# LayerNorm, causal attention and a ternary feed-forward block: gate and up of a batch in seven block products of 256 columns instead of eight

## The chip, the cores and the metric

The kernel runs on one core of a Trainium2 chip. A core has TensorE (matmul, called PE; its weight loads are shown as PEld), VectorE (DVE), ScalarE (ACT), GpSimd (POOL) and SyncE (SP), which run side by side and wait for each other by semaphores; SP, ACT and POOL also issue DMAs. Matmuls write to PSUM; the kernel's pools divide it into eight banks of 512 fp32 columns. The metric is the device time of one execution in microseconds (us), taken as the median of several runs.

## The reference

For x of 4 batches, 512 positions and 512 features:

```
xn = layernorm(x)                                   # per position, no scale or shift
s  = causal_attention(xn)                           # 16 heads of 128, W_Q, W_K, W_V, W_O, biases
g  = (xn @ gate_w.T) * gate_s                       # gate_w, up_w: 1408 x 512, entries -1, 0, 1
u  = (xn @ up_w.T) * up_s
f  = silu(((silu(g) * u) @ down_w.T) * down_s)      # down_w: 512 x 1408, entries -1, 0, 1
out = x + s * f
```

All is fp32. The kernel keeps fp32 accuracy by splitting an activation into a high part (rounded to fp32r, the type of the matmuls' operands) and the rest, a low part; a matrix of small whole numbers needs no low part.

## The kernel before

The x of all batches lies normalised and transposed in SBUF (`xnT`, per batch a high and a low tile of 128 x 4 x 512: four chunks of 128 features, 512 positions). The kernel has two stages, both with the order of instructions written out by hand (`manual_schedule`): on each engine they stand in the order in which the Python code issues them.

**Attention.** 64 heads (8 groups of 2 heads, 4 batches) run one after the other, each with scores and softmax (`softmax`), a transpose of p through VectorE and DRAM (`turn_p`, on SP's queue), the projection of the next head's q and k (`project`), v (`project_v`) and the output projection (`project_out`, which adds to `acc_d` in DRAM through the tiles `a`, in the last batch `a_last`, stored by SP at L499). GpSimd scales p (L371) and makes low halves of weights. Once a head, `look` ORs one tile of the ffn's weights into `bits` on VectorE (L529) and `load_look` loads the next on ScalarE's queue, 33 tiles in all: low bits in any of them would mean weights that need a low part. The answer is read into a register (L843), and the branch takes the exact path when there are none, which holds for these inputs.

**ffn.** `gate_up(b, f)` is called for 4 batches and 11 blocks f of 128 hidden features (L776). GpSimd's queue loads the two weight blocks (`fweight`, L754, six buffers each) and, in the second half of batch 0, the down weights `wd`. Per block, gate and up are 8 matmuls each of 128x128 weights by 512 columns (`mm`, L770: 4 chunks, high and low part), into PSUM tiles pg and pu of which there are two each. ScalarE makes silu(gate) (L794), VectorE multiplies with up (L796), ScalarE rounds to the high part (L800), VectorE subtracts for the low part (L801). After the first block of the next batch come the four tiles of `down` (L814): 22 matmuls of 512 columns each, and on the way out a product (L825, VectorE), a silu (L826, ScalarE), a product with the attention (L827) and the addition of x (L828), then SP's store (L829). Two PSUM banks hold the downs. The last batch's downs end the kernel, the last tile in two halves.

Of the kernel before, what the change touches and what calls it, by code (L numbers as in the profile page):

```python
# [10 lines left out]
F32 = mybir.dt.float32  # L11
F32R = mybir.dt.float32r
I32 = mybir.dt.int32
# [15 lines left out]
class Split:  # L29


    def __init__(self, hi, lo):
        self.hi, self.lo = hi, lo
# [10 lines left out]
def kernel(  # L44
# [44 lines left out]
    ]  # L89

    def mm3(ps, a, b, first, last):
        nc.tensor.matmul(ps, a.hi, b.lo, start=first, stop=False)  # L92
        nc.tensor.matmul(ps, a.hi, b.hi, start=False, stop=False)  # L93
        nc.tensor.matmul(ps, a.lo, b.hi, start=False, stop=last)  # L94
# [16 lines left out]

    with ExitStack() as at:
        lnp = at.enter_context(tc.tile_pool(name="lnp", bufs=NT))
        small = at.enter_context(tc.tile_pool(name="small", bufs=8))
# [17 lines left out]

        ident = const.tile([P, P], F32, name="ident")
        mask = const.tile([P, S], F32, name="mask")
        eps = const.tile([P, 1], F32, name="eps")

        def load_const(src, shape, name):
            t = const.tile(shape, F32, name=name)
            nc.gpsimd.dma_start(out=t, in_=src)
            return t  # L140
# [128 lines left out]

        v_of = {}  # L270

        def project_v(g, b, t):
# [6 lines left out]
            else:  # L279
# [8 lines left out]
                for c in range(ND):  # L288
                    nc.tensor.matmul(  # L289
                        ps[:, 1], x_[c].lo, wv[g].hi[:, c, :], start=False, stop=c == ND - 1  # L290
                    )
                rest = lnp.tile([P, D], F32, name="v_rest", tag="xn")[:, : HG * E]
                nc.scalar.copy(v.hi, ps[:, 0])
# [217 lines left out]

        n_ffn = 3 * NF
        bits = const.tile([P, D], I32, name="bits")
        looks, looking = list(range(n_ffn)), []

        def load_look():
            if looks:
                k = looks.pop(0)
                src = (gate_w, up_w, down_w)[k % 3][k // 3]
                if k % 3 < 2:  # L520
                    src = src.rearrange("p c i -> p (c i)")
                raw = lnp.tile([P, D], F32, name=f"look{k}", tag="xt")
                nc.scalar.dma_start(out=raw, in_=src)
                looking.append(raw)

        def look():
            if looking:
                raw = looking.pop(0)
                nc.vector.tensor_tensor(bits, bits, raw.bitcast(I32), ALU.bitwise_or)  # L529

        def low_bits():

            nc.vector.tensor_single_scalar(bits, bits, LOW_BITS, ALU.bitwise_and)
            low = const.tile([P, 1], F32, name="low")
            nc.vector.tensor_reduce(low, bits, AX.X, ALU.max)
            return low
# [9 lines left out]
        with tc.manual_schedule():  # L546
# [11 lines left out]
            nc.gpsimd.memset(bits, 0)  # L558
            ones = const.tile([P, 1], F32, name="ones")
            nc.gpsimd.memset(ones, 1.0)  # L560
# [41 lines left out]
            project_v(0, 0, 1)  # L602
            bo_bc = load_const(b_o.broadcast_to([P, D]), [P, D], "bo_bc")
            ds_bc = load_const(down_s.broadcast_to([P, D]), [P, D], "ds_bc")

            load_on[0] = nc.scalar
            heads = [(g, b, i) for g in range(NG) for b in range(B) for i in range(HG)]
            zs = {}
# [7 lines left out]
            for n, (g, b, i) in enumerate(heads):  # L616
# [69 lines left out]
                if g + 1 < NG:  # L686
# [5 lines left out]
                    if (b, i) == (B - 1, 0):  # L692
                        prepare_qk((g + 1) * HG + 1, (g + 1) * per_g - 1)
                look()
                if g > 0:
                    load_look()
                if before is not None:
# [22 lines left out]
                if n == len(heads) - 4:  # L720
                    assert not looks and not looking
                    low = low_bits()
# [7 lines left out]

# [110 lines left out]
    with tc.If(flag == 0) as cond:  # L844
        ffn(True)
    with cond.Else():
# [60 lines left out]
```

## Time and profile before

| what | us |
|---|---|
| median of 3 runs (1206.56 to 1209.08) | 1207.38 |
| the profiled execution | 1208.75 |
| its span, first to last instruction | 1207.0 |
| start of the ffn on TensorE | 960.23 |
| end of the last matmul's turn on TensorE | 1200.15 |
| from there to the end of the span | 6.85 |
| busy in the ffn's 239.92 us: TensorE / VectorE / ScalarE | 239.91 / 95.81 / 68.75 |

The profile is one execution. Rows of the chain and of timelines give a start from the beginning of the span and a length in us, then engine, line (L770 is line 770 of the kernel), operation, output<-inputs by name, shape and count; brackets give how long the engine had idled and what ended that. Rows of groups give the busy time and the mean ns of one. Matmuls overlap: one of 512 columns is shown 389 ns long, but starts follow each other more closely.

### The profile page before, as it was taken

How to read it: one execution, taken by the hardware profiler on the slowest of the kernel's cores; microseconds unless marked ns; L12 is line 12 of the kernel's file. 1: busy time of each engine (PE TensorE's matmuls, PEld its weight loads, DVE VectorE, ACT ScalarE, POOL GpSimd, SP SyncE). 2: the span in 40 equal slices, each digit the busy share in tenths (PEclk: the TensorE clock that was granted, in tenths of full speed). 3: DMA queues.
4: the chain of work that ended last, by engine and by line, in shares of the span. 5: the costliest groups of instructions: out<-in, count | busy, mean ns of one | idle time of the engine just before them, and what ended most of it. 6: DMA issues, size and time to landing. Idle time of an engine off the chain costs nothing.

```text
span 1207.0 us, 18482 instructions
## 1 busy us (share of the span) xinstructions
PE 1194.2 (99%) x6018; PEld 1021.9 (85%) x6018; DVE 841.8 (70%) x2261; ACT 549.8 (46%) x1272; POOL 366.9 (30%) x484
## 2 busy tenths in 40 slices
PE   8999999999999999999999999999999999999997
PEld 8888888888888888888888888888888888888886
DVE  7987778787778777777777777777777543443433
ACT  6654444455445545444544454555544331323231
POOL 3312332343235323332523252335231350202110
PEclk9999999999999999999999999999999999999999
DMA  4465456666665667666766665655555992737241
GB/s 163 141 186 149 145 163 206 196 191 193 192 209 180 204 196 220 183 198 201 218 186 183 182 191 171 187 176 175 175 159 169 299 297 80 218 79 219 78 149 38
DMA packets 117912, 215.52 MB, mean 179 GB/s; under 512 B 13232, under 2 KB 45744, under 8 KB 117808
## 3 DMA queue, kind: packets, MB, share of 16 engines
q1 hardware_dynamic: 73872, 134.38, 35.2%
q10 hardware_dynamic: 29520, 53.40, 15.7%
q0 software_dynamic: 14416, 26.48, 8.2%
q8 instruction: 50, 0.82, 0.3%
q14 instruction: 54, 0.44, 0.1%
HBM read 135.17 MB, written 79.04 MB: 177 GB/s over the span
## 4 chain that ended last, share of the span: by engine, by line
PE 94%; DVE 3%; DMA 1%; ACT 1%; issue 0%; SPq 0%; ACTq 0%; DVEq 0%
PE psq L104 14%; PE psk L104 14%; PE psv L285 9%; PE z L452 8%; PE sc L104 8%; PE pd L770 7%; PE pg L770 7%; PE pu L770 7%; PE pso L92 5%; PE pso L93 5%; PE pso L94 5%; PE psv L289 4%; PE psv L104 1%; PE sc L342 1%; DVE sq L385 1%; DVE st L213 1%
## 5 line engine op out<-in xcount | busy, mean ns | idle before, releaser
L371 POOL TENSOR_SCALAR p<-p,rtot 128x512 f32<-128x512 f32 (+3 forms) x256 | 135.3, 547 | 603.0 <-DVE rtot L368 578.6
L365 ACT ACTIVATE p<-p,nmax 128x512 f32<-128x512 f32 (+3 forms) x256 | 140.8, 552 | 137.3 <-DVE nmax L351 137.3
L285 PE MATMUL psv<-wv,xh 128*128 128x512 f32 x448 | 124.7, 400 | 0.0
L104 PE MATMUL sc<-k,q 128*128 128x512 f32 (+2 forms) x576 | 112.6, 338 | 2.5 <-DVE xl L261 1.8
L385 DVE STREAM_TRANSPOSE sq<-p 128x256 f32<-128x256 f32 x378 | 113.4, 365 | 0.0
L104 PEld LDWEIGHTS sc<-k,q 128*128 128x128 f32 x576 | 99.0, 188 | 14.3 <-ACT xh L260 1.5
L351 DVE CUSTOM_DVE_ANT_0 p<-sc,mask 128x512 f32<-128x512 f32 (+2 forms) x192 | 96.3, 552 | 0.0
L308 ACT ACTIVATE k<-psk,consts 128x512 fp32r<-128x512 f32 (+1 forms) x65 | 44.3, 681 | 106.0 <-PE psk L104 106.0
L418 ACT CAST pt<-ptr 128x640 fp32r<-128x640 f32 x126 | 85.1, 724 | 13.2 <-DMA ptr<-turn 8.5
L309 DVE SCALAR_TENSOR_TENSOR k<-psk,consts,k 128x512 fp32r<-128x512 f32 (+1 forms) x65 | 48.1, 740 | 61.2 <-ACT k L308 60.8
L420 POOL TENSOR_TENSOR pt<-ptr,pt 128x640 fp32r<-128x640 f32 x53 | 83.7, 1579 | 13.3 <-ACT pt L418 10.3
L285 PEld LDWEIGHTS psv<-wv,xh 128*128 128x128 f32 x448 | 76.0, 188 | 10.0
L796 DVE SCALAR_TENSOR_TENSOR hd<-pu,consts,sg 128x512 f32<-128x512 f32 x44 | 33.0, 751 | 66.8 <-PE pu L770 62.2
L289 PEld LDWEIGHTS psv<-wv,xl 128*128 128x128 f32 x448 | 68.4, 188 | 9.5
L420 DVE TENSOR_TENSOR pt<-ptr,pt 128x640 fp32r<-128x640 f32 x73 | 69.9, 968 | 3.0 <-ACT pt L418 3.0
L498 DVE TENSOR_TENSOR a<-pso,a 128x512 f32<-128x512 f32 x108 | 69.8, 685 | 3.0 <-PE sc L343 1.7
L289 PE MATMUL psv<-wv,xl 128*128 128x256 f32 x448 | 71.0, 280 | 0.0
L368 DVE RECIPROCAL rtot<-tot 128x1 f32<-128x1 f32 x256 | 41.4, 162 | 41.2 <-ACT p L365 35.1
L308 ACT ACTIVATE q<-psq,consts 128x512 fp32r<-128x512 f32 (+1 forms) x65 | 44.2, 681 | 42.4 <-PE psq L104 41.8
L452 PE MATMUL z<-pt,v_0h 128*128 128x512 f32 x128 | 50.6, 395 | 0.0
L309 DVE SCALAR_TENSOR_TENSOR q<-psq,consts,q 128x512 fp32r<-128x512 f32 (+1 forms) x65 | 47.8, 735 | 3.9 <-ACT q L308 3.9
L365 ACT ACTIVATION_READ_ACCUMULATOR p<-p,nmax 128x1 f32 x256 | 47.8, 187 | 0.0
(717 smaller groups left out, 3037.3 us busy)
## 6 DMA issues: line engine op xcount, KB each, us to landing
turn<-sq SPq DMA_DIRECT2D x63, 640.0 KB, 2.9
ptr<-turn SPq DMA_DIRECT2D x252, 160.0 KB, 5.2
acc<-a SPq DMA_DIRECT2D x124, 256.0 KB, 2.5
a<-acc ACTq DMA_DIRECT2D x108, 256.0 KB, 3.3
xt<-in_x SPq DMA_DIRECT2D x16, 256.0 KB, 4.3
wor<-in_w_o ACTq DMA_DIRECT2D x16, 256.0 KB, 6.2
fa<-acc SPq DMA_DIRECT2D x16, 256.0 KB, 5.8
fx<-in_x SPq DMA_DIRECT2D x16, 256.0 KB, 5.9
```

The costliest lines, as they stand in the source:

```text
L104: nc.tensor.matmul(ps, l, r, start=n == 0, stop=n == len(todo) - 1)
L285: nc.tensor.matmul(ps, x_[c].hi, wv[g].both[:, :, c, :], start=c == 0, stop=False)
L289: nc.tensor.matmul(ps[:, 1], x_[c].lo, wv[g].hi[:, c, :], start=False, stop=c == ND - 1)
L308: nc.scalar.activation(q.hi[:, at_], ps, AF.Identity, bias=bias[:, h : h + 1])
L309: nc.vector.scalar_tensor_tensor(q.lo[:, at_], ps, bias[:, h : h + 1], q.hi32[:, at_], ALU.add, ALU.subtract)
L351: nc.vector.tensor_tensor_reduce(out=of[t], in0=where[t], in1=add, scale=-SCALE, scalar=BIG, op0=ALU.add, op1=ALU.min, accum_out=nmax[t],)
L365: nc.scalar.activation(of[t], of[t], AF.Exp, bias=nmax[t], scale=-1.0, accum_out=tot)
L371: nc.gpsimd.tensor_scalar(of[t], of[t], rtot, 1.0, ALU.mult, ALU.mult)
L385: nc.vector.transpose(dst.rearrange("p a s i -> p s a i"), src.rearrange("p (s a i) -> p s a i", s=n, i=Q),)
L420: on.tensor_tensor(dst(pt.lo), src, dst(pt.hi32), ALU.subtract)
L452: nc.tensor.matmul(o, v, p_, start=k == 0, stop=k == len(todo) - 1)
L770: nc.tensor.matmul(ps, l, r, start=first and k == 0, stop=last and k == len(pairs) - 1)
```

## The change

Take the weights of a block as a 2x2 matrix of blocks (gate and up by the first and second half of the features: g1, g2, u1, u2) and a batch of x likewise (b11, b12, b21, b22: halves of features by halves of positions). Gate and up of the batch are the product of both, which takes eight block products; the new code forms sums of blocks and takes seven, after Winograd. The weights' sums s1 to s4 are small whole numbers; x's sums t1 to t4 are split anew into high and low.

The attention makes the weights' sums: `look` and `load_look` become `chores`, one step a head. In four heads it loads gate and up of a block, ORs gate and makes the four sums of 128x256 on GpSimd while it loads the down block, ORs up and the first sums tile and stores both tiles through SP into `sum_d`, and ORs the second. The sums are looked at as well. `v_rest` becomes one tile for all calls; constants of the attention alone move to a pool that ends with it.

The ffn of exact weights is new, `ffn_exact`; the other path stays. Each unit (b, f) is a list of pieces with a time in slots, seven slots to a unit; pieces with times past 7 fall into the next units, and a list sorted by time issues them. `plain` is the old pair of products, in two slots' positions; PLAIN says how many units of each batch are so (4, 1, 0, 0). `seven` is the new form. Its PSUM tile px collects four products in turn, copied out by ScalarE after the first three (s1, u2, u3); pz takes two, py one. VectorE adds the pieces: sg0 (gate, first half of positions), c22, sg1 (gate, second half). c22 must be read from pz before the product in slot 11 adds to it.

`sums_of(b)` makes x's sums: 13 steps on VectorE of 128x512 and 4 roundings on ScalarE. For batch 0 they stand among its plain units, for batch 1 all at once ahead of the first down, for batches 2 and 3 one at slots 2.5 and 5.5 of the units f = 2 to 8 of the batch before. A unit loads, on GpSimd's queue, gate, half of up and the sums (896 KB instead of 512), in batch 0 one down block more after each unit's own weights.

```diff
--- before.py
+++ after.py
+    sum_d = [dram.tile([P, 2 * D], F32, name=f"sum{f}", tag=f"sum{f}") for f in range(NF)]
...
-                rest = lnp.tile([P, D], F32, name="v_rest", tag="xn")[:, : HG * E]
+                if not v_rest:
+                    v_rest.append(lnp.tile([P, D], F32, name="v_rest", tag="xn"))
+                rest = v_rest[0][:, : HG * E]
...
-        def load_look():
...
-        def look():
...
+        def chores():
+            sums = [lnp.tile([P, D], F32, name=f"sums{k}", tag="xn") for k in range(2)]
+            h_ = D // 2
+            d = []
+            for f in range(NF):
+                g = load_look(gate_w[f].rearrange("p c i -> p (c i)"), f"lookg{f}")
+                u = load_look(up_w[f].rearrange("p c i -> p (c i)"), f"looku{f}")
+                look(*d)
+                yield
+                look(g)
+                s1, s2, s3, s4 = (t[:, c : c + h_] for t in sums for c in (0, h_))
+                for o, l, r, op in (
+                    (s1, u[:, :h_], u[:, h_:], ALU.add),
+                    (s2, s1, g[:, :h_], ALU.subtract),
+                    (s3, g[:, :h_], u[:, :h_], ALU.subtract),
+                    (s4, g[:, h_:], s2, ALU.subtract),
+                ):
+                    nc.gpsimd.tensor_tensor(o, l, r, op)
+                d = [load_look(down_w[f], f"lookd{f}")]
+                yield
+                look(u, sums[0])
+                for k in range(2):
+                    nc.sync.dma_start(out=sum_d[f][:, ts(k, D)], in_=sums[k])
+                yield
+                look(sums[1])
+                yield
+            look(*d)
+            found.append(True)
...
-                look()
                 if g > 0:
-                    load_look()
+                    next(chore)
...
+    def ffn_exact():
...
+            ps_y = ff.enter_context(tc.tile_pool(name="ps_y", bufs=1, space=PSUM))
+            ps_z = ff.enter_context(tc.tile_pool(name="ps_z", bufs=2, space=PSUM))
+            ps_d = ff.enter_context(tc.tile_pool(name="ps_d", bufs=2, space=PSUM))
+            N2, D2 = S // 2, ND // 2
+            PLAIN = (4, 1, 0, 0)
...
+            def sums_of(b):
+                (b11, b12), (b21, b22) = blk[b]
...
+                steps = (
+                    (p, b12.hi32, b11.hi32, ALU.subtract),
+                    (q, low(b12), low(b11), ALU.subtract),
+                    (p, p, q, ALU.add),
+                    (t1, p),
+                    (q, b22.hi32, p, ALU.subtract),
+                    (q, q, low(b22), ALU.add),
+                    (t1.lo, p, t1.hi32, ALU.subtract),
+                    (t2, q),
+                    (p, b21.hi32, q, ALU.subtract),
+                    (p, p, low(b21), ALU.add),
+                    (t2.lo, q, t2.hi32, ALU.subtract),
+                    (t4, p),
+                    (q, q, b11.hi32, ALU.subtract),
+                    (q, q, low(b11), ALU.subtract),
+                    (t4.lo, p, t4.hi32, ALU.subtract),
+                    (b12, q),
+                    (b12.lo, q, b12.hi32, ALU.subtract),
+                )
+                for o, *of in steps:
+                    if len(of) == 1:
+                        nc.scalar.copy(o.hi, *of)
+                    else:
+                        dve(o, *of)
+                        yield
...
+            def load_down(k):
+                wd[k] = wdp.tile([P, D], F32R, name=f"wd{k}", tag=f"wd{k}")
+                nc.gpsimd.dma_start(out=wd[k], in_=down_w[k])
+            def load(src, shape, tag, bufs=None):
+                t = fw.tile(shape, F32R, name=tag, tag=tag, **({"bufs": bufs} if bufs else {}))
+                nc.gpsimd.dma_start(out=t, in_=src)
+                return t
+            def product(ps, w, x_, more=False):
+                todo = [
+                    (w[:, c, :], part[:, c, :])
+                    for part in (x_.hi, x_.lo)
+                    for c in range(w.shape[1])
+                ]
+                for k, (l, r) in enumerate(todo):
+                    nc.tensor.matmul(
+                        ps, l, r, start=not more and k == 0, stop=k == len(todo) - 1,
+                        skip_group_check=more,
+                    )
+            def leave_hid(b, hd):
+                s = Split(
+                    hp.tile([P, S], F32R, name="hh", tag="hh"),
+                    hp.tile([P, S], F32R, name="hl", tag="hl"),
+                )
+                hid.setdefault(b, []).append(s)
+                nc.scalar.copy(s.hi, hd)
+                yield
+                nc.vector.tensor_tensor(s.lo, hd, s.hi32, ALU.subtract)
+            def times(o, up, f, sg):
+                nc.vector.scalar_tensor_tensor(
+                    o, up, us_sb[:, f : f + 1], sg, ALU.mult, ALU.mult
+                )
...
+            def plain(b, f):
+                g = load(gate_w[f], [P, ND, P], "wg")
+                u1 = load(up_w[f][:, :D2], [P, D2, P], "wu1", 2)
+                u2 = load(up_w[f][:, D2:], [P, D2, P], "wu2", 4)
+                pg = ps_x.tile([P, S], F32, name="pg", tag="x")
...
+            def seven(b, f):
...
+                g = load(gate_w[f], [P, ND, P], "wg")
+                u2_ = load(up_w[f][:, D2:], [P, D2, P], "wu2", 4)
+                s_ = load(sum_d[f][:, : 3 * D2 * P].rearrange("p (c i) -> p c i", i=P),
+                          [P, 3 * D2, P], "ws")
+                s4 = load(sum_d[f][:, 3 * D2 * P :].rearrange("p (c i) -> p c i", i=P),
+                          [P, D2, P], "ws4", 4)
+                s1, s2, s3 = (s_[:, k * D2 : (k + 1) * D2] for k in range(3))
+                px = ps_x.tile([P, N2], F32, name="px", tag="x")
+                pz = ps_z.tile([P, N2], F32, name="pz", tag="z")
+                made = {}
+                def temp(name):
+                    made[name] = fp.tile(
+                        [P, N2], F32, name=name, tag=name, bufs=1 if name in ("s1", "u3") else 2
+                    )
+                    return made[name]
+                def plus(o, ps, t):
+                    nc.vector.tensor_tensor(temp(o), ps, made[t], ALU.add)
+                def at0():
+                    product(px, g[:, :D2], b11)
+                    nc.scalar.copy(temp("s1"), px)
+                def at1():
+                    py = ps_y.tile([P, N2], F32, name="py", tag="y")
+                    product(py, g[:, D2:], b21)
+                    plus("sg0", py, "s1")
+                def at3():
+                    product(px, s2, t2, True)
+                    nc.scalar.copy(temp("u2"), px)
+                    silu(made["sg0"], f)
+                def at5():
+                    product(pz, s1, t1)
+                def at6():
+                    product(px, s3, t3, True)
+                    nc.scalar.copy(temp("u3"), px)
+                def at8():
+                    plus("c22", pz, "u3")
+                def at9():
+                    product(px, u2_, t4, True)
+                    made["hd"] = fp.tile([P, S], F32, name="hd")
+                def at10():
+                    times(made["hd"][:, :N2], px, f, made["sg0"])
+                def at11():
+                    product(pz, s4, b22, True)
+                    plus("sg1", pz, "u2")
+                def at13():
+                    silu(made["sg1"], f)
+                def at14():
+                    times(made["hd"][:, N2:], made["c22"], f, made["sg1"])
+                    made["left"] = leave_hid(b, made["hd"])
+                def at16():
+                    next(made["left"])
+                def at17():
+                    next(made["left"], None)
+                return [
+                    (0, at0), (1, at1), (3, at3), (5, at5), (6, at6), (8, at8), (9, at9),
+                    (10, at10), (11, at11), (13.5, at13), (15.5, at14), (17.5, at16), (19, at17),
...
+            class Down:
+                def __init__(self, b, t, c=slice(0, D), store=nc.sync, o=None):
+                    self.b, self.t, self.c, self.store = b, t, c, store
+                    self.o = fp.tile([P, D], F32, name="o") if o is None else o
+                    self.ps = ps_d.tile([P, c.stop - c.start], F32, name="pd", tag="pd")
+                def add(self, ff_):
+                    for f in ff_:
+                        h_ = hid[self.b][f][:, ts(self.t, P)]
+                        for part in (h_.hi, h_.lo):
+                            nc.tensor.matmul(
+                                self.ps, part, wd[f][:, self.c],
+                                start=f == 0 and part is h_.hi,
+                                stop=f == NF - 1 and part is h_.lo,
+                            )
+                    return self
+                def leave(self, last=True):
+                    a, xt = tail_in[self.b, self.t]
+                    silu_product(self.o, self.ps, self.c, a, xt)
+                    self.store.dma_start(
+                        out=out[self.b, ts(self.t, P), self.c], in_=self.o[:, self.c]
+                    )
...
+                units = [(b, f) for b in range(B) for f in range(NF)]
+                for k, (b, f) in enumerate(units):
+                    at_ = 7 * k
+                    if b > 0 and f == 1:
+                        run(at_)
+                        for e in [e for e in events if e[2] == k - 2]:
+                            events.remove(e)
+                            e[1]()
+                        if b == 1:
+                            sums = sums_of(b)
+                            advance()
+                        for t in range(NT):
+                            Down(b - 1, t).add(range(NF)).leave()
+                            if t + 3 < NT:
+                                load_tail(b - 1, t + 3)
+                    if f < PLAIN[b]:
+                        unit = plain(b, f)
+                        if b == 0:
+                            advance((6, 3, 2, 1)[f])
+                    else:
+                        if b == 0 and f == PLAIN[b]:
+                            advance()
+                        unit = seven(b, f)
+                    if b == 0:
+                        load_down(f)
+                    if 0 < b < B - 1 and f == 2:
+                        sums = sums_of(b + 1)
+                    if 0 < b < B - 1 and 2 <= f < 9:
+                        unit = sorted(
+                            unit + [(2.5, lambda: advance(1)), (5.5, lambda: advance(1))],
+                            key=lambda e: e[0],
+                        )
+                    events += [(at_ + n, what, k) for n, what in unit]
+                    run(at_ + 7)
+                    if f == NF - 1:
+                        for t in range(3):
+                            load_tail(b, t)
...
-        ffn(True)
+        ffn_exact()
```

## The prediction

> **What bounds the kernel now.** I began with the busy times of the page:
>
> ```profile
> PE 1194.2 (99%) x6018; PEld 1021.9 (85%) x6018; DVE 841.8 (70%) x2261; ACT 549.8 (46%) x1272; POOL 366.9 (30%) x484
> ```
>
> TensorE works 99% of the span, so time is won only by giving it less to do, and lost by every gap opened on it. Next the chain that ended last, in order of time, for the ffn:
>
> ```profile
> 960.23 2.08 PE pg L770 x8
> 962.31 1.81 PE pu L770 x8
> 964.13 1.81 PE pg L770 x8
> ...
> 1004.02 19.95 PE pd L770 x88
> ...
> 1179.91 20.24 PE pd L770 x110
> ```
>
> The ffn begins at 960.2; a gate or an up of 8 matmuls of 512 columns takes 1.813 us (226.7 ns each), the four tiles of a down 19.95. Nothing stands between these rows. What a 256-column matmul costs back to back is in the timeline of TensorE near the start:
>
> ```profile
> 13.77 0.64 PE L104 MATMUL psv<-wv,xh 128*128 128x256 f32 x4
> ...
> 18.09 0.64 PE L104 MATMUL psv<-wv,xh 128*128 128x256 f32 x4
> 18.57 0.40 PE L104 MATMUL sc<-k,q 128*128 128x512 f32 x1
> ```
>
> Forty start between 13.77 and 18.57: 4.80/40 = 120 ns. (The last down agrees: 20.24 less 66 x 0.2267 leaves 5.28 for 44, 120 ns.) Half the columns cost 53% of the time.
>
> Three more views set the prices of gaps. First the weight queue (timeline of POOL) and, below it, SP's stores of the last attention sums:
>
> ```profile
> 956.28 0.53 POOL L754 DMA_DIRECT2D wu5h<-in_up_w  x1 [0.45 <-DMA wu1h<-in_up_w]
> 965.41 0.53 POOL L754 DMA_DIRECT2D wd0h<-in_down_w  x1 [8.60 <-DMA fx<-in_x]
> ```
> ```profile
> 955.89 4.44 SPq L499 DMA_DIRECT2D acc<-a_last  x4
> ```
>
> The first down weight, wd0, lies where the attention's last tiles lay: it waits 8.6 us, until the stores of `a_last` (last issue 960.0) have landed. Today twelve gate and up loads stand ahead of it in the queue. Then VectorE and ScalarE after the last tile of a down (timelines):
>
> ```profile
> 1083.85 0.69 DVE L825 TENSOR_TENSOR o<-pd,ds_bc 128x512 f32<-128x512 f32 x1 [2.18 <-PE pd L770]
> 1085.23 0.69 DVE L827 TENSOR_TENSOR o<-o,fa 128x512 f32<-128x512 f32 x1 [0.70 <-ACT o L826]
> 1085.96 0.69 DVE L828 TENSOR_TENSOR o<-o,fx 128x512 f32<-128x512 f32 x1
> ```
> ```profile
> 1084.57 0.63 ACT L826 ACTIVATE o<-o 128x512 f32<-128x512 f32 x1 [4.36 <-DVE o L825]
> ```
>
> TensorE left the down at 1083.64; VectorE is held by this chain until 1086.65, 3.0 us, ScalarE until 1085.20. Today nobody needs them. Last, a 256-wide addition out of PSUM (groups, shapes apart):
>
> ```profile
> L294 DVE TENSOR_TENSOR v_rest<-psv,v_0h 128x256 f32<-128x256 f32 x25 | 10.6, 425 | 2.3
> ```
>
> [...] here the granted clock fell about 2.7 us after the last matmul. A gap of 3.9 could pay for that[...]; it goes into the range.
>
> **The change part by part.** *Products.* A plain pair has 16 x 226.7 = 3.63 us; seven products of 4 matmuls have 28 x 120 = 3.36. PLAIN keeps 4+1 pairs, so 39 change: 39 x 0.266 = **-10.4 us**. Downs, tail and last output are as before.
>
> *Attention.* 33 looks become 55 (22 x 0.75 = 16.5 us of VectorE), there are 44 sums of 128x256 on GpSimd and 22 stores on SP. A head lasts 14.6 us of unbroken TensorE; in 600 to 629 us VectorE was busy 23.7 of 29.2. Five looks in four heads instead of four add 0.2 us a head, at most 0.75 at once. The sums follow the weight halves in GpSimd's queue and precede the next head's scaling of p, for which GpSimd waits 603 us in all; at 1.58 us for 640 (pt, L420) four of 256 are 2.5 us, an estimate. SP's stores wait for sums made one head earlier. I take 0; at worst an uncovered look in eleven heads, +8, which nothing suggests.
>
> *(a) Start.* The queue is now gate, up, up, wd0 of unit 0, and only then unit 1's gate. wd0 still waits for `a_last`, but with three loads instead of twelve ahead the stores should land in 2.5 us (the median of acc<-a), near 962.5. Unit 1's gate issues at 963 and lands after the 2.9 to 3.0 us of an uncrowded load: 966. TensorE wants it at 960.2 + 3.63 = 963.9. Gap **2.0 us**: at least 1.0 (a store of 2.0), at most 5 (wd0 at 965.4 as today).
>
> *(b) x's sums of batch 1.* All 13 VectorE steps are issued ahead of the first down's output. From the end of the plain unit (T0): its two products, a cast and a subtraction, and the last seven unit's product, cast and subtraction, reach T0+4.2. Thirteen steps at 0.61 to 0.73 (most read what the step before wrote) end at 13.2; the first down then leaves PSUM at 13.8. The third down needs that bank (two of them) at T0+10.0. Gap **3.9**, 2.5 to 5. What is late next, the second down's exit at 16.5, precedes the fourth down's need at 18.9.
>
> *(c) Joints after a down.* With the 3.0 us chain at the head of both queues: ScalarE's copy s1, needed before the fourth product of the unit, ends at 1.9 instead of 1.05, so that product starts at 2.0 instead of 1.44; the eleventh-slot product next needs VectorE's c22, which starts at 3.0 and ends 3.4: another 1.0. So 1.6 for batches 2 and 3; for batch 1, whose previous unit is plain, only s1 and u2: 1.1. **4.3**, from 2 to 5.
>
> *(d) x's sums of batches 2 and 3 among the products.* A seven unit asks VectorE for three additions (0.425), two products (0.49, extrapolated from 618 ns for 384 and 749 for 512) and one subtraction of 0.69: 2.94. In the trace waiting instructions start about 0.08 before the one ahead ends (three L498 in 1.88 us): 2.46. Two x-sums of 0.61 make 3.68 against 3.36: 0.32 late per unit, for 6.5 units 2.1, of which about 0.7 fits into the time by which u3 and c22 come early. **1.4 a batch, 2.8**. Below: 0. Without overlap 4.32: 0.96 x 6.5 - 0.5 = 5.7 a batch, 11.4. ScalarE has three copies (0.37), two silus (0.47), one cast (0.62): 2.67 of 3.36, hidden.
>
> *(e) Latencies in a unit.* A product's result is out 0.64 us after its start, a copy takes 0.37 and two slots are 0.96; where a silu lies ahead of s1 the margin is 0.15. I take 0.3 for the first seven unit and 0.6 for the rest, **0.9**; 0 to 4.
>
> *DMA.* Four or five issues of 0.53 us a unit: 2.7 of 3.36. In batch 0 a unit loads 1152 KB = 1.18 MB, 3.0 us at the 390 GB/s seen between 960 and 983: hidden; at 292 GB/s (mean of 960 to 1000) 4.04, +0.68 x 7.
>
> Sum: -10.4 + 2.0 + 3.9 + 4.3 + 2.8 + 0.9 = **+3.5 us**. The profiled execution took 1208.75 (span 1207.0 and 1.75 around it): 1212.3. The median of the runs is 1.37 lower: **1210.9**.
>
> **The rivals.** *VectorE keeps up* (other side): x's sums cost nothing, (b) and (d) vanish, -3.2: 1204.2. It decides where the sums cost under 3.2 us in all (the rest of the gaps is 7.2 against 10.4). For it: the down leaves VectorE 13 us of 20. Against: 0.69 a step, and the order of the queue. *VectorE becomes the bound*: no overlap, (d) 11.4: 1219.5. Against: starts closer than durations. *Weights become the bound in batch 0*: +4.8: 1215.7. For it: DMA was busy 98% from 960 to 1000; against: TensorE did not wait then. *256 columns don't pay*: bound by the 188 ns of a weight load, 28 x 0.188 = 5.26, +64 us; the 120 ns rule it out.
>
> **How the numbers follow.** Forecast 0.45 (by itself 1207 to 1214), VectorE keeps up 0.27, VectorE the bound 0.13, weights 0.12, others 0.03. The range 1203 to 1219 leaves out the quickest part of the second and the slowest of the last. 0.2% (2.4 us) is about what can be told from no change. Faster 0.28 (most of the second case, a little of the first), same 0.14, slower 0.58.
>
> **What would show it.** Rows of 28 matmuls in 3.36 us; a gap of about 2 us before unit 1's gate, with wd0 issued near 962.5; one of about 4 before the third down of batch 0, released by o<-pd; two of 0.5 and 1.0 after each later down, released by s1 and c22; VectorE over 95% busy while sums run. An unbroken TensorE at these places, a 256-column matmul far from 120 ns, or a longer attention would make it wrong.

## The result: 1.1% slower, where 0.3% was forecast

| what | before | after |
|---|---|---|
| median, us | 1207.34 (1206.56 to 1209.08) | 1221.35 (1220.01 to 1222.06) |
| ratio to before | | 1.0113, interval 1.0098 to 1.0128 |
| profiled execution / its span, us | 1208.75 / 1207.0 | 1221.51 / 1219.7 |
| start of the ffn on TensorE | 960.23 | 960.02 |
| first gate matmul to last matmul, starts | 239.63 | 253.00 |
| from the start of the last matmul to the end | 7.12 | 6.72 |

The direction was right and the time was not: 1221.35 lies above 1210.9 and above the range's end, 1219. The attention is as long as before; all of the loss is in the ffn. One of the five runs of `wd_late` below took 3029.11 us, for a reason that is not known, and stays out of its median. On the page TensorE is still busy 98% of the span, but the row of the granted clock has an 8 in two places of the ffn:

```profile
PE 1194.8 (98%) x6486; PEld 1040.9 (85%) x6486; DVE 944.8 (77%) x2496; ACT 599.8 (49%) x1449; POOL 447.3 (37%) x611
...
PEclk9999999999999999999999999999999898999999
```

TensorE's waits in the ffn of the changed kernel (engine, line, what it waited for: total, times, longest, in us):

```profile
PE pg L874 <- DMA wg<-in_gate_w: 5.4, 1, 5.4
PE pd L1025 <- DVE o L766: 4.0, 2, 3.7
PE px L874 <- ACT s L953: 2.8, 4, 1.5
PE pz L874 <- DVE c L949: 1.6, 2, 0.8
```

These are the waits that the prediction names in (a), (b), (c) and (e). The first is far longer than forecast. To size each place with what follows it, I took the starts of all matmuls of the ffn and subtracted 0.2267 us for each of 512 columns and 0.120 for each of 256; what is left over is lost time.

| place | forecast | left over in the trace |
|---|---|---|
| 39 units in seven products | -10.4 | -10.4 |
| (a) before unit 1's gate | 2.0 | 5.5, and 1.9 in the matmuls after it |
| (b) before the third down of batch 0 | 3.9 | 3.8, and 3.0 in the matmuls after it |
| (c) joints after a down, batches 1, 2, 3 | 1.1, 1.6, 1.6 | 1.2, 1.6, 1.6 |
| (d) units with x's sums | 1.4, 1.4 | 1.0, 1.1 |
| (e) other units | 0.9 | 2.0, all in unit (0,4) |
| end, last batch's downs | 0 | 0.8 |
| sum | +3.5 | +13.1 |

The ffn grew by 13.4. The chain of waits of the changed kernel shows the start:

```profile
962.53 0.52 POOL wd L859
963.05 6.18 DMA wg<-in_gate_w
...
969.27 3.78 PE pg L874 x8
973.06 1.93 PE pu L874 x8
974.99 1.82 PE pg L874 x8
...
978.62 1.81 PE pg L874 x8
...
990.51 0.48 PE py L874 x4
...
993.87 0.48 PE py L874 x4
```

The lower rows give the first row of the table: a plain unit takes 978.62 - 974.99 = 3.63 us and a seven unit 993.87 - 990.51 = 3.36 where nothing interrupts them, and 39 units have changed.

wd0 went out at 962.53 and unit 1's gate at 963.05, as forecast (962.5 and 963). But the gate took 6.18 us to land, not 3.0. And its 8 matmuls took 3.78 us where eight of a later unit took 1.82: half speed. At the third down the same chain has

```profile
1024.38 0.69 DVE o L766
...
1025.12 13.10 PE pd L1025 x44
...
1076.40 19.99 PE pd L1025 x88
```

Two tiles of a down cost 13.10 us, where four of the next batch cost 19.99, so two should cost 10.0. Busy times by stretch (columns: stretch, length, busy time and instructions of PE, PEld, DVE, ACT, POOL, then granted clock, DMA share, GB/s) say why:

```profile
1021.00:1024.00 3.00, 0.44 (x2) 0.01 (x1) 2.79 (x5) 1.24 (x2) 0.00 (x0) 1.00 0.00 0
1024.00:1026.00 2.00, 0.89 (x2) 0.79 (x3) 1.30 (x3) 0.63 (x1) 0.00 (x0) 0.57 0.00 0
1026.00:1029.00 3.00, 3.00 (x8) 2.33 (x8) 2.27 (x4) 0.63 (x1) 0.00 (x0) 0.50 0.26 90
...
1031.00:1034.00 3.00, 3.00 (x15) 2.45 (x14) 0.69 (x1) 0.02 (x1) 0.00 (x0) 0.98 0.16 59
```

TensorE idles from 1021.4 on, the clock halves at 1024.3, and it stays at 0.50 until 1031.1, 6 us after work has resumed; 8 matmuls fall into 3 us where 15 do after 1031. "Busy" hides this: a slow matmul counts as busy. So there are two open questions: why the gate landed late, and whether the half speed is the price of the gap before it.

### The profile page after: what moved, and what is told of

It reads as the page before. It is cut to its first block, busy times and chain, and to the rows that moved or that the text cites. A ratio compares the mean times of both kernels' runs of the same rounds, so it can differ in the third digit from the quotient of the medians.

```text
span 1219.7 us, 20216 instructions
## 1 busy us (share of the span) xinstructions
PE 1194.8 (98%) x6486; PEld 1040.9 (85%) x6486; DVE 944.8 (77%) x2496; ACT 599.8 (49%) x1449; POOL 447.3 (37%) x611
## 5 line engine op out<-in xcount | busy, mean ns | idle before, releaser
L427 DVE TENSOR_TENSOR pt<-ptr,pt 128x640 fp32r<-128x640 f32 x73 | 76.6, 1060 | 2.6 <-ACT pt L425 2.6
L1025 PE MATMUL pd<-wd,hh 128*128 128x512 f32 (+1 forms) x187 | 71.6, 388 | 4.0 <-DVE o L766 4.0
L1025 PE MATMUL pd<-wd,hl 128*128 128x512 f32 (+1 forms) x187 | 71.3, 386 | 0.0
L863 POOL DMA_DIRECT2D ws<-sum x78 | 41.6, 543 | 36.4 <-PE px L874 33.4
L863 POOL DMA_DIRECT2D wg<-in_gate_w x44 | 24.0, 546 | 78.2 <-PE py L874 68.1
```

Of the source, the lines that this page charges most:

```text
L427: on.tensor_tensor(dst(pt.lo), src, dst(pt.hi32), ALU.subtract)
L1025: nc.tensor.matmul(self.ps, part, wd[f][:, self.c], start=f == 0 and part is h_.hi, stop=f == NF - 1 and part is h_.lo,)
```

## The experiments

Medians below stand beside 1221.35 of the changed kernel. The ratios stand against the kernel before on the same chip: 1207.98 for the first four kernels told of here, 1207.29 for `joints`, `unit_04` and `tuned_2`, 1207.68 for the rest. The kernel before thus moves by 0.7 us from chip to chip, and differences of less than about 1 us between medians are not read here.

### The start: place in the queue or crowded engines

```diff
-                    if b == 0:
-                        load_down(f)
+                    if b == 0 and f > 1:
+                        for j in (2 * f - 4, 2 * f - 3) if f < 4 else (f,):
+                            load_down(j)
```

> One edit to the changed kernel: in batch 0 the first down weight is loaded after the weights of unit 2 and not after those of unit 0 (two each in units 2 and 3, one in each later unit). Theory, place in the queue: unit 1's gate waits only because it stands behind wd0, which waits for the stores of a_last. Then the gap of 5.5 us before unit 1's gate goes, and with it the half clock that follows it (1.9 us): 1221.35 - 7.4 = 1213.9 us. Rival, crowding: the DMA engines are full from 960 to 975 whatever the order, because fa and fx and the weights come together; then unit 2's up (whose tile is free only at 964) is late in place of unit 1's gate, by 2 to 5 us: 1216 to 1221.

Measured: 1213.67, -7.7; ratio 1.0045 (1.0029 to 1.0061). The gap before unit 1's gate is gone, and nothing came in its place at unit 2. So without the gate's place behind wd0 there is no gap. (The profiled execution also lost 1.7 us more in unit (0,4), where the clock now fell, and 1.2 less than the changed kernel after the third down.) What made 5.5 of the forecast 2.0 is the question of the next run.

```diff
             def load_tail(b, t):
+                queue = nc.gpsimd if b == 0 and t < 3 else nc.sync
                 a = fa.tile([P, D], F32, name="fa")
-                nc.sync.dma_start(out=a, in_=acc_d[b][t])
+                queue.dma_start(out=a, in_=acc_d[b][t])
                 xt = fa.tile([P, D], F32, name="fx")
-                nc.sync.dma_start(out=xt, in_=x[b, ts(t, P), :])
+                queue.dma_start(out=xt, in_=x[b, ts(t, P), :])
```

> One edit to the changed kernel: the six loads of fa and fx for batch 0's downs (1.57 MB, issued by SyncE from 960.5 on) go to GpSimd's queue, behind the last weights of batch 0; wd0 stays ahead of unit 1's gate. It takes the landing time apart from the queue's place. If the 6.2 us that unit 1's gate needed from issue to landing come of sharing the DMA engines with fa and fx, it lands in the 3.0 us that I had predicted, at 966.1: gap 2.3 instead of 5.5, [...]so 3.2 + 1.9 = 5.1 us less: 1216.2. If they come of GpSimd's own five loads in a row, the gate still lands after 968 and the time stays within 1 us of 1221.3.

Measured: 1219.27 (1216.39 to 1220.68), -2.1. The order of wd0 and the gate is untouched. Timelines of GpSimd and, below it, of TensorE in this run, at the start and at the end of batch 0:

```profile
962.55 0.55 POOL L863 DMA_DIRECT2D wg<-in_gate_w  x1
```
```profile
962.78 0.61 PE L874 MATMUL pu<-xl,wu 128*128 128x512 f32 x2
965.68 1.19 PE L874 MATMUL pg<-xh,wg 128*128 128x512 f32 x4 [2.28 <-DMA wg<-in_gate_w]
...
1004.12 1.20 PE L874 MATMUL pg<-xh,wg 128*128 128x512 f32 x4 [2.68 <-DMA wg<-in_gate_w]
```

The gate, issued at 962.55, is there by 965.68: 3.1 us, the 3.0 that I had used, and TensorE waits 2.28 us for it, with no fall of the clock (the gate's eight matmuls then take 1.95 us, not 3.78). In the six profiles in which SyncE's six loads run beside it (the changed kernel, `sums_spread`, `warm_gap`, `no_sums_2_3`, `joints`, `unit_04`) this wait is 4.6 to 5.9. SyncE's timeline in the changed kernel shows these loads, the first and the last of the six:

```profile
960.48 0.32 SPq L1008 DMA_DIRECT2D fa<-acc  x1
...
962.83 0.36 SPq L1010 DMA_DIRECT2D fx<-in_x  x1
```

All six, of 256 KB each, are out before the gate's issue at 963.05. The gate needs 6.18 us with these six ahead of it and 3.1 without them, though they were issued by another engine. The run won only 2.1 because the six loads now stand ahead of unit (1,0)'s gate in GpSimd's queue: the second wait above, 2.68 us. Forecast 5.1 less this 2.7 makes 2.4.

### The third down: x's sums, and the half speed after the gap

```diff
                         if b == 1:
                             sums = sums_of(b)
-                            advance()
                         for t in range(NT):
-                            Down(b - 1, t).add(range(NF)).leave()
+                            d = Down(b - 1, t).add(range(NF))
+                            if b == 1:
+                                advance((5, 4, 4, 0)[t])
+                            d.leave()
```

> One edit to the changed kernel: the 13 VectorE steps of batch 1's x sums stand five ahead of the first down's exit, four ahead of the second's and four ahead of the third's, instead of all 13 ahead of the first. Theory: the gap of 3.8 us before the third down, and the half clock after it (another 2.95 us), go: 1221.35 - 6.8 = 1214.6. Rival: VectorE has too much in this stretch in any order (13 steps of 0.65 and four exits of 2.75 us on 20 us of TensorE), and the wait moves to the fourth down or to the first products of the next unit: 2 to 4 us of the 6.8 come back, 1216.5 to 1218.5.

Measured: 1216.56, -4.8; ratio 1.0069 (1.0052 to 1.0086). The down is unbroken at full clock; busy times by stretch of this run:

```profile
1015.00:1020.00 5.00, 5.00 (x24) 4.14 (x23) 4.10 (x7) 1.57 (x4) 0.00 (x0) 1.00 0.21 56
1020.00:1025.00 5.00, 5.00 (x24) 4.14 (x23) 4.20 (x7) 1.33 (x3) 0.00 (x0) 1.00 0.08 30
```

So VectorE has room for the 13 steps here, in another order. Of the 6.8 us 1.0 came back at the joint behind it (2.2 left over instead of 1.2: the last exits start later), and in the profiled execution the start lost 0.5 more than in that of the changed kernel. And the 2.95 of half clock in the forecast was read from one execution. In four other profiles that have the same gap of 3.7 to 3.8 us (`wd_late`, `tail_behind`, `no_sums_2_3`, `joints`) it cost 1.7: there the clock was low for 3.41 us and not for 6.83. With 1.7 the forecast is 1221.35 - 5.5 + 1.0 = 1216.9.

```diff
                         for t in range(NT):
+                            if b == 1 and t == 2:
+                                warm = ps_x.tile([P, S], F32, name="warm", tag="x")
+                                for _ in range(14):
+                                    nc.tensor.matmul(
+                                        warm, wd[0][:, :P], wd[0], start=True, stop=True
+                                    )
                             Down(b - 1, t).add(range(NF)).leave()
```

> One edit to the changed kernel: 14 matmuls of 512 columns whose result nobody reads stand ahead of batch 0's third down, where TensorE idles 3.8 us (14 x 0.227 = 3.2 us). The wait for the first down's exit is left as it is. If the half speed of the 13 matmuls after this gap is the clock's answer to the idle time, the gap is filled, the clock stays and 2.9 us go: 1218.4. If something else slows them (the loads of the next weights run at the same time), nothing is won: 1221.3, or a little more where the extra matmuls run past the end of the wait.

Measured: 1219.12, -2.2; ratio 1.0094 (1.0077 to 1.0110). Timeline and stretches of this run:

```profile
1020.48 3.33 PE L1068 MATMUL warm<-wd 128*128 128x512 f32 x14
1024.32 0.50 PE L1025 MATMUL pd<-wd,hh 128*128 128x512 f32 x1 [0.51 <-DVE o L766]
```
```profile
1026.00:1030.00 4.00, 4.00 (x19) 3.29 (x19) 2.72 (x5) 0.63 (x1) 0.00 (x0) 1.00 0.58 194
```

The wait for the down's exit still ends when it did. With TensorE kept busy meanwhile the clock stays at 1.00 and the third down runs at full speed, while the same weights are loaded. The half speed is the answer to the idle time, shown by this run. That the median moved by 2.2 and not by 2.9 fits two things: the fall costs 1.7 in some executions, and in this profile the units after the joint lost 0.8 more than in the changed kernel, waiting for weights.

### Do the two add up, and do seven products pay

The kernel `both` has the edits of `wd_late` and `sums_spread`.

> The edits of wd_late and sums_spread together. If the two gaps are independent, the gains add: 1221.35 - 7.1 - 4.8 = 1209.5 us, still no faster than the kernel before. If one had been hidden behind the other (a core that idles once anyway), it is 1212 or more. The gap of 1.5 to 1.8 us in unit (0,4) is left in; where it lets the clock fall, 1.7 us more.

Measured: 1209.67, ratio 1.0016 (1.0009 to 1.0023). The gains add within the noise (7.7 + 4.8 = 12.5; 11.7 measured), and without the two gaps the change is about even. The 20 runs also show the clock at work: this kernel keeps two waits of 1.7 and 1.8 us, at unit (0,4) and at the joint after batch 0's downs. The six runs with a mean granted clock of 0.999 have a median of 1208.5, the seven with 0.996 one of 1210.7. In the profiled execution, one of the six, the clock does not fall within the ffn.

`all_plain` has the loads' order of `wd_late` and

```diff
-            PLAIN = (4, 1, 0, 0)
+            PLAIN = (NF,) * B
...
-                            advance((6, 3, 2, 1)[f])
+                            pass
...
-                            sums = sums_of(b)
-                            advance()
+                            pass
...
-                    if 0 < b < B - 1 and f == 2:
+                    if False:
...
-                    if 0 < b < B - 1 and 2 <= f < 9:
+                    if False:
...
-                events, sums = [], sums_of(0)
+                events, sums = [], iter(())
```

> PLAIN is 11 for every batch and no sums of x are made: the new attention, the new order of loads (first down weight behind unit 2, as in wd_late) and the new code of the ffn, but all products in the old form. If the seven products alone give 39 x 0.266 = 10.4 us, and the attention costs nothing, this kernel is the kernel before: 1207.5 within 1.5 us. If the attention's chores cost what I had as the worst case, it is up to 8 us above that; if 256 columns did not pay, it would be 10 us or more under the time of the kernel with seven products and no gaps.

Measured: 1208.88, ratio 1.0011 (1.0002 to 1.0020): 1.2 us over the kernel before, of which the trace shows 0.6 at the end, where the last batch's first down is finished behind ten blocks of the second. The attention's chores are as good as free. Against the kernel `tuned` below, the ffn (starts, first gate to last matmul) takes 240.85 here and 234.41 there: 6.4 us less, on the same chip. By the unit times above, seven products save 10.4. The difference is what TensorE still waits there: 5.3 us are left over in `tuned` and 1.3 in `all_plain`, by the same prices of a matmul (so this is the same reading in another form, and no second measurement of the 10.4).

### The smaller terms

```diff
-                for o, *of in steps:
+                for o, *of in steps if b < 2 else ():
```

> The changed kernel without the x sums of batches 2 and 3 (26 steps on VectorE, 8 roundings on ScalarE left out; the products of these batches read what the tiles held before). It sizes step (d). Read from the trace of the changed kernel, 2.1 us are lost in the units that carry them: 1219.2. By the prediction's middle 2.8: 1218.5. If VectorE were the bound there, 11.4: 1210.

Measured: 1218.84, -2.5. VectorE is not the bound in these units. The 2.5 can't be taken for the size of (d), though: in the profiled execution the ffn starts 1.4 us earlier than in that of the changed kernel, within the spread of the attention. In the units themselves 1.4 is left over where there were 2.1, and 0.9 of it is one new wait for the weights' sums. So (d) is 2.1 at most, by the trace.

In `joints` the exit of the last down of a batch is four events among those of the next unit:

```diff
+                def parts(self, at_, k):
...
+                    return [
+                        (at_ + 0.4, lambda: tt(o[:, c], self.ps, ds_bc[:, c], ALU.mult), k),
+                        (at_ + 1.5, lambda: nc.scalar.activation(o[:, c], o[:, c], AF.Silu), k),
+                        (at_ + 3.2, lambda: tt(o[:, c], o[:, c], a[:, c], ALU.mult), k),
+                        (at_ + 4, end, k),
+                    ]
...
-                            Down(b - 1, t).add(range(NF)).leave()
+                            d = Down(b - 1, t).add(range(NF))
+                            if t == NT - 1:
+                                events += d.parts(at_, k)
+                            else:
+                                d.leave()
```

> One edit to the changed kernel: the exit of a batch's last down is cut into its four pieces, which stand between the pieces of the next unit, behind s1 and c22. Theory (step (c)): the waits at the three joints come only from the order of VectorE's and ScalarE's queues, 1.2 + 1.6 + 1.6 = 4.4 us: 1221.35 - 4.4 = 1216.9. Rival: VectorE and ScalarE have no room there, and the pieces make the same products late: within 1.5 us of 1221.3.

Measured: 1218.16, -3.2. The order of the queues was the cause: TensorE's waits in this run have no line for c22 any more, and s1 is waited for once, in unit (0,4). But there is a new line among them:

```profile
PE px L874 <- DMA ws<-sum: 1.4, 3, 0.6
```

The sums of the weights, for which nobody waited in the profile of the changed kernel, come late in three units. So part of what the joints gave comes back at the next thing that is late (2.2 us are left over in the units that follow the second joint, where there were 1.1).

```diff
-                    for _ in leave_hid(b, hd):
-                        pass
-                return [(1, gate), (5, up)]
+                    gated.append(leave_hid(b, hd))
+                return [
+                    (1, gate), (5, up),
+                    (7.5, lambda: next(gated[2])), (9, lambda: next(gated[2], None)),
+                ]
...
-                        if b == 0 and f == PLAIN[b]:
-                            advance()
                         unit = seven(b, f)
+                        if b == 0 and f == PLAIN[b]:
+                            unit = sorted(unit + [(2, advance)], key=lambda e: e[0])
```

It was made for unit (0,4), where ScalarE's timeline in the changed kernel reads

```profile
983.27 0.62 ACT L885 CAST hh<-hd 128x512 fp32r<-128x512 f32 x1 [1.90 <-DVE hd L890]
983.79 0.61 ACT L850 CAST xh<-tq 128x512 fp32r<-128x512 f32 x1
984.31 0.36 ACT L953 COPY s<-px 128x256 f32<-128x256 f32 x1
```

Two roundings, the first waiting for a product, stand ahead of the copy s1 that unit (0,4) needs.

> One edit to the changed kernel: the rounding and the subtraction of a plain unit stand behind s1 of the next unit, and batch 0's last x sum with its rounding in slot 2 of unit (0,4). Theory (step (e), under-sized): the wait of 1.5 us and its sequels in unit (0,4), 2.0 us in the trace, come from the two roundings ahead of s1 in ScalarE's queue: 1219.3; up to 1 us less, since in batch 1 the plain unit's subtraction also leaves VectorE's queue ahead of the x sums. Rival: s1 waits for px itself: no change, 1221.3.

Measured: 1217.46, -3.9, more than expected, and for another reason. In unit (0,4) the wait for s1 is gone, but the two roundings now delay u2: 1.1 of the 2.0 stay. In batch 1, though, the same edit takes a rounding and a subtraction out of the way of x's sums: the gap before the third down shrinks from 3.8 to 2.5, and no half speed follows. 1.3 + 3.0 + 0.9 would be 5.2; with 1.7 for the half speed, as in four other profiles, it is the 3.9 that the median shows.

### The edits together

`tuned` has the edits of `wd_late`, `sums_spread`, `joints` and `unit_04` and finishes the last batch's first down behind seven blocks of the second instead of ten.

> Five edits to the changed kernel: the first down weight behind unit 2; batch 1's x sums spread over the downs' exits; the exit of a batch's last down cut into four pieces that stand between the pieces of the next unit (so that s1 and c22 stand ahead of its silu and its second product); the last plain unit's rounding and batch 0's last x sum behind s1 of unit (0,4); the last batch's first down ended earlier among the second's matmuls. By the gaps that I read in the trace: 1221.35 - 7.1 - 5.8 - 2.0 (unit (0,4)) - 1.2 - 1.6 - 1.6 (joints) - 0.7 (end) = 1201.4. If VectorE has no room for the exit in the first unit after a down, about 1 us comes back at each of three joints: 1204.5.

Measured: 1202.36, **0.9958 of the kernel before (0.9941 to 0.9975)**. TensorE's waits in its ffn are one line:

```profile
PE px L874 <- DMA ws<-sum: 1.0, 3, 0.5
```

`tuned_2` moves x's sums of batches 2 and 3 among the downs too, makes the first units of these batches plain and spreads the down weights differently.

> The kernel tuned, with two more edits: the x sums of batches 2 and 3 also stand among the exits of the downs (for which their first unit is plain, 2 x 0.27 us), none among the products; and one down weight a unit from unit 3 on, so that unit 4's sums of weights come earlier. In the trace of tuned the units with x sums lose 1.3 us and late sums of weights in unit 4 some 1.4. Theory: VectorE has room for 13 steps in each down, so 1202.4 - 1.3 - 1.4 + 0.5 = 1200.2. If it has not, the second to fourth down of batches 2 and 3 wait, 2 us or more each: 1204 or more.

Measured: 1204.16, ratio 0.9978 (0.9967 to 0.9989), missed by 4 us. No down of batches 1 to 3 waits, so VectorE had the room; but the late sums of weights moved: in unit (0,4) nobody waits for them any more, and TensorE waits 1.6 us for them elsewhere, once 1.4, at 1093.2 in batch 2. The trace of `tuned_2` has two things ahead of this wait. GpSimd's queue stood until 1086.60 for a product, so that these sums went out at 1088.68; and SyncE had issued six loads of fa and fx from 1084.59 to 1086.97, as at the start of the ffn. In `joints` and `tuned` two of the three late sums come at the same place, behind the same six loads. Which of the two is the cause was not tested.

## Why the prediction was right or wrong

**Products, attention.** Right: 3.63 and 3.36 us for a unit, by which seven products save 10.4, and an attention that starts the ffn within its usual spread (958.6 to 961.6 in all profiles). The sentence "Downs, tail and last output are as before" missed 0.8 at the end.

**(a), the step that failed most.** The mechanism and both issue times were right. The term that was mis-sized is "lands after the 2.9 to 3.0 us of an uncrowded load". The load was not uncrowded: fa and fx go out on SyncE from 960.5, and I had them in the same view of the kernel before, as the releaser of wd0's wait ("DMA fx<-in_x"). 6.18 us instead of 3.0 makes the gap 5.5 instead of 2.0; `tail_behind` gave the 3.1 back. I counted the queue that the gate stands in, and not the six loads that SyncE had issued just before it. My upper end of 5 came from another case (wd0 as late as before) and did not cover it.

**The clock, the second failure.** "A gap of 3.9 could pay for that", and it went into the range alone. It was not a could: in all profiles together the clock fell after each of the eleven gaps of 3.67 us or more. In the four other profiles with the third down's gap the fall lasts 3.41 us and costs 1.7; in the changed kernel's profiled execution both falls lasted 6.83, and cost 3.0 after the third down's gap and 1.9 after the start's. Together with (a)'s excess of 3.5 this is 8.4 of the 9.6 us missing from the sum. With 1.7 for the gap of 3.9 in the sum, the forecast would have been 1212.6 and the range's end 1220.7, still just short of 1221.35. (The reading of the kernel before is a little off: from the end of the last matmul's turn, 1200.15, to the fall at 1202.68 it is 2.5 us, not 2.7.)

**(b) and (c).** Right to 0.1 us in each gap, from queue order and durations alone; `sums_spread`, `joints` and `tuned` show that the order, not the amount of work, made them.

**(d) and (e).** (d) 2.8 against 2.1 in the trace; without the overlap of starts it would have been 11.4, which `no_sums_2_3` rules out. (e) 0.9 against 2.0: I gave 0.3 to the first seven unit as if it followed another, and did not walk through ScalarE's queue there.

**Rivals.** VectorE as the bound is excluded by `no_sums_2_3`. VectorE keeping up is excluded for the order as written and is what `tuned` shows for a better one. Weights as the bound in batch 0, +4.8: no load is waited for in batch 0's later units in the changed kernel; where the other gaps are gone, in `tuned`, 1.4 us are lost in units (0,4) and (0,5), of which 0.5 is a wait for the weights' sums.

## What to carry to other kernels

The gap before the third down had two prices: its length of 3.8 us, and 3.0 (in four other profiles 1.7) in the half-clock matmuls after it. Put both into the sum. In these profiles the clock fell after all eleven gaps of 3.67 us or more, and after two of the thirteen between 1.5 and 2.7. When a load's landing time decides, list what all queues have issued in the microseconds before it: the same gate took 6.18 us behind six loads of another queue and 3.1 without them, so a bare duration from a quiet stretch does not carry over. This schedule was lost not by the amount of work on the helper engines but by the order of their queues: with the same work in another order `sums_spread` took 4.8 us less and `joints` 3.2. Walk through each queue at every seam, the first and last units above all.

## What the runs showed of the clock

Within each profile all falls and rises of the granted clock lie a whole number of 3.413 us apart. In the changed kernel they stand at 966.26, 973.09, 1024.29 and 1031.12, and the fall after the last matmul at 1215.43: 1024.29 - 966.26 = 58.03 = 17 x 3.413, and 1215.43 - 966.26 = 249.17 = 73 x 3.413. So I cut each profile at these distances into steps of 3.413 us. Within the ffn a half-clock stretch lasts one step or two (3.41 or 6.83 us). Which of the two goes with the rest of the gap: where it still took 0.83 us or more of the first half-clock step the next was at half speed too (six stretches), and where it took 0.40 or less the clock came back (seven). At the third down of the changed kernel it took 0.83, from the fall at 1024.29 to the first matmul at 1025.12. So the same gap of 3.7 to 3.8 us before the third down could cost 3.0 us in one profile and 1.7 in four: the edge of a step cut it at another place.

In `wd_late` a gap of 1.82 us in unit (0,4) was followed by a fall. Its stretches, cut at the edges of the steps:

```profile
974.64:978.05 3.41, 1.59 (x13) 1.38 (x12) 2.53 (x6) 1.65 (x4) 2.57 (x6) 1.00 1.27 386
978.05:981.46 3.41, 3.41 (x17) 3.23 (x16) 0.61 (x2) 1.28 (x4) 2.60 (x5) 0.50 1.13 306
```

TensorE is busy 1.59 us of the first step, so it idles 1.82, and the next ran at a granted clock of 0.50. Counted so over the ffn in all profiles, every full-speed step with 2.37 us idle or more was followed by one at half speed, and none with 1.40 or less. Between them it went both ways: 1.53 (`no_sums_2_3`) and 1.82 (`wd_late`) were followed by one, 1.71 (`both`) and 1.82 (`tail_behind`) were not. So these profiles show no single limit between 1.40 and 2.37 us, and idle time as the profile models it does not decide the cases between.

Where an edge cuts a gap differs from gap to gap: in the changed kernel the clock fell 2.37 us after TensorE had stopped at 963.89, and 2.85 us after it had stopped at 1021.44. That the runs of `tail_behind` spread by 4.3 us fits this: its two quicker runs have a mean granted clock of 0.998, the two slower ones 0.995. Which gap the clock answered in them is not known, since only one was profiled.
